# Spectral layers 2 and 3: wider matmuls for two tiles, a turned x transform, 1 MB transfers on two queues, another hand-written order

## The chip, the cores and the metric

The kernel runs on one core of a Trainium2 chip. The metric is the device time of one launch in microseconds, lower is better. All arithmetic is fp32. Engines are named as in the profile: PE is TensorE's matmul stream (PEld its weight loads), DVE is VectorE, ACT is ScalarE, POOL is GpSimd and SP is SyncE. DMA transfers are issued by SP, POOL or ACT and carried by the core's 16 DMA engines.

## The reference

64 images of 256x256 pass a Fourier neural operator of four layers with 32 channels. Its result, 256 tokens of 256 values, gets 77 text tokens appended, and one transformer layer follows (attention, then a feed-forward over about half of the tokens). The change touches only the operator's layers, so the rest is left out:

```python
v = jnp.transpose(h @ p_w + p_b, (0, 3, 1, 2))
for i in range(4):
    W1 = fw1[i, ..., 0] + 1j * fw1[i, ..., 1]
    W2 = fw2[i, ..., 0] + 1j * fw2[i, ..., 1]
    x1 = _fourier_layer(v, W1, W2)       # rfft2, mix 24 x 12 modes over channels, irfft2
    x2 = jnp.einsum('bcxy,cd->bdxy', v, w_w[i]) + w_b[i][None, :, None, None]
    v = x1 + x2
    mean = jnp.mean(v, axis=(0, 2, 3), keepdims=True)
    var = jnp.var(v, axis=(0, 2, 3), keepdims=True)
    v = (v - mean) * jax.lax.rsqrt(var + BN_EPS) * bn_g[i] + bn_b[i]
    if i < 3:
        v = jax.nn.relu(v)
out = jnp.einsum('bcxy,cu->bxyu', v, q_w) + q_b
```

The mean and variance run over all 64 images, so a layer can't be normalised before its whole batch is known.

## The kernel before

The feature map v of an image is 8 MB and goes through HBM between layers. A layer is split in two. `mix` multiplies the few kept Fourier modes by the layer's weights, finds mean and variance from them and from sums of squares, and writes the mixed modes to HBM (`mix_d`). Then `layer(i, ...)` is a pass over the 64 images: it builds the layer's output, applies the normalisation and ReLU, and in the same sweep takes the forward transform of the result and the sums of squares of the next layer. There are three such passes (i = 0, 1, 2; "pass 1, 2, 3" below). Pass 1 needs no feature map as input (it is linear in x); passes 2 and 3 load it. After them the transformer stage loads the map once more.

An image is eight tiles t = 0..7 of 128 partitions (four groups of 32 channels) by 8 rows by 256 columns, 1 MB each. In a pass these steps run, each a small function of `layer`:

- `ld` loads a tile into one of four `vin` buffers: two DMAs on SP, 512 KB each (L661). `am` loads an image's mixed modes into `ams` (two DMAs on SP, L626) and scales them with two POOL instructions (L634).
- `sp` (two halves of an image) turns the modes into rows by a matmul (L667); `spT` transposes them on DVE (L675).
- `pre` makes a tile: eight matmuls of 24 rows from the modes (L687) and sixteen 32x32 ones from `vin` (L698) into four PSUM banks. `evA` and `evB` each evict two of the banks with ReLU into one of four `vo` buffers, on ACT (suffix `.a`, L710) or on DVE (`.d`, L712).
- `st` stores the tile from `vo` to HBM: two DMAs on SP, 512 KB each (L719). `turn` transposes it on DVE into `t32` (L724).
- `prod` multiplies the tile by the next layer's channel weights: sixteen 32x32 matmuls, row group n into bank n (L735). `sqA`, `sqB` square and sum the result on ACT (L746).
- `y0`..`y7`, after all eight tiles of an image, transform along y (L757); `half` (ACT, L767), `zt0` and `zt1` (DVE, L775) carry the result out. `x` transforms along x in twelve matmuls (L791), `xo` copies on ACT (L802), `xs` stores the modes on SP (L808).

PSUM is four pairs of banks, `ring0` to `ring3`. `take` gives the pairs that were closed earliest in program order, `close` marks the step that frees one. `pre`, `prod` and `y` take two pairs, `sp` and `x` one; `y` holds its two from `y0` until `half` and `zt0`.

What sets the order is a string written out by hand, `ORDER[0]` for pass 1 and `ORDER[1]` for passes 2 and 3: a loop over images b emits the steps word by word, `@k` shifts a word to image b + k. No scheduler moves them (`manual_schedule`), so each engine and each queue executes its steps in the order of the string, and waits where its inputs or buffers are not ready. A buffer of `vo` is free again when its tile's store, `turn` and `prod` are done, one of `vin` when its `pre` is done. DMAs of one issuing engine share eight completion semaphores in turn, so a DMA also waits for the one issued eight before it.

Of the kernel before, what the change touches and what calls it, by code (L numbers as in the profile page):

```python
# [9 lines left out]
F32 = mybir.dt.float32  # L10
# [7 lines left out]
C = 32  # L18
M = 12
KX = 2 * M  # L20
# [14 lines left out]
def _tables():  # L35
# [92 lines left out]
ORDER = [(  # L128
# [7 lines left out]
), (  # L136
# [7 lines left out]
)]  # L144

_TABLES, _GRIDS = _tables()
# [7 lines left out]
def tile_fno_fusion_transformer(ctx: ExitStack, tc: tile.TileContext, a, cst_d, grid_d, out):  # L154
    nc = tc.nc
    x = a["x"].rearrange("b x y o -> b x (y o)")
# [3 lines left out]
    const = ctx.enter_context(tc.tile_pool(name="const", bufs=1))  # L160
# [15 lines left out]
    T4, ID, ONES, CHAN = tab("t4"), tab("ident"), tab("ones"), tab("chan")  # L176

    CROW = tab("crow").rearrange("p (n k) -> p n k", n=4)

    epsc = const.tile([128, 1], F32, name="epsc")  # L180
    nc.vector.memset(epsc, EPS)

# [29 lines left out]
    w4 = [w4all[:, i, :] for i in range(L)]  # L212
# [336 lines left out]
    def layer(i, st, src, dst, acc):  # L549
# [3 lines left out]
        EX, FX = EXL[lay], FXL[lay]  # L553
# [3 lines left out]
        with ExitStack() as cx:  # L557
            def pool(name, bufs, **kw):
# [3 lines left out]
            op, yp, cp, xp, zp, tp = (  # L562
                pool(n, k, reuse_waits="tile")
                for n, k in (("lo", 4), ("ly", 1), ("lc", 1), ("lx", 2), ("lz", 1), ("lt", 6))
            )
# [20 lines left out]
            for n in range(nr):  # L586
# [4 lines left out]
                if n:  # L591
                    nc.vector.tensor_add(a0, a0, a1)
            nc.vector.tensor_copy(ams[1], ams[0])
            ws = cp.tile([128, C], F32, name="ws")
            if i:
                nc.vector.tensor_mul(ws, w4[i], s_)
            if i == 0:
                mv = [ip.tile([128, 4, 4 * S + 8], F32, name="mv") for n in range(2)]
                mv = [t[:, :, 0:4 * S].rearrange("p q (s y) -> p q s y", s=4) for t in mv]
                for t in mv:  # L600
                    nc.sync.dma_start(t, grid_d.rearrange("p (q s y) -> p q s y", q=4, s=4))

            ring, free, clock = {}, [0] * 4, [0]

            def take(key, n):

                clock[0] += 1
                mine = sorted((k for k in range(4) if free[k] >= 0), key=lambda k: free[k])[:n]
                for k in mine:
                    free[k] = -1  # L610
                ring[key] = [(k, pp.tile([128, 2, 512], F32, name=f"ring{k}")) for k in mine]
                return [t for _, t in ring[key]]

            def banks(key):
                return [t[:, n] for _, t in ring[key] for n in range(2)]
# [6 lines left out]
            y_, t32, vin, vo, half_, zts = {}, {}, {}, {}, {}, {}  # L622

            def load_am(b):
                for n in range(2):
                    nc.sync.dma_start(  # L626
                        ams[b % 2][64 * n:64 * n + 2 * KX],
                        mix_d[i][:, :, :, b].rearrange("p m k c -> (p m k) c")[:, 512 * n:512 * n + 512],
                    )

            def scale_am(b):
                for _, p0, cs in halves:
                    v = ams[b % 2][p0:p0 + 2 * KX].rearrange("p (c k) -> p c k", k=32)
                    nc.gpsimd.tensor_tensor(  # L634
                        v, v,
                        s_[p0:p0 + 2 * KX, cs].rearrange("p (c o) -> p c o", o=1)
                        .to_broadcast([2 * KX, 16, 32]), ALU.mult,
                    )
# [7 lines left out]
            def am(b, n, e):  # L646
                if b > 1:
                    load_am(b)
                    scale_am(b)

            def lx(b, n, e):
# [3 lines left out]
            def ld(b, t, e):  # L655
                if (b, t) in vin:
                    return
                vin[b, t] = ip.tile([128, 8, S], F32, name="vin")
                for n in range(2):
                    rows = slice(4 * n, 4 * n + 4)  # L660
                    nc.sync.dma_start(vin[b, t][:, rows], src[b][:, t, rows])  # L661

            def sp(b, h, e):
                ps = take(("sp", b, h), 1)[0]
# [49 lines left out]
                return run  # L714

            def st_(b, t, e):
                for n in range(2):
                    rows = slice(4 * n, 4 * n + 4)
                    nc.sync.dma_start(dst[b][:, t, rows], vo[b, t][:, rows])  # L719
# [9 lines left out]
            def prod(b, t, e):  # L729
                take(("prod", b, t), 2)  # L730
                ps = banks(("prod", b, t))
                for k in range(4):
                    for n in range(4):
                        j = (n + k) % 4
                        nc.tensor.matmul(  # L735
                            ps[n][32 * j:32 * j + 32], lhsT=w4[i + 1][32 * n:32 * n + 32],
                            rhs=vo[b, t][32 * n:32 * n + 32, 2 * j:2 * j + 2, :], start=True, stop=True,
                            skip_group_check=True, tile_position=(32 * n, 32 * j),
                        )

            def sq(n):
                def run(b, t, e):
                    key = "prod", b, t
                    at = 2 * (8 * b + t) + n
                    ps = ring[key][n][1]
                    nc.scalar.activation(ps, ps, AF.Square, accum_out=acc[:, at:at + 1])  # L746
                    close(key, n)
                return run
# [21 lines left out]
            def zt(h):  # L770
                def run(b, n, e):
                    if b not in zts:
                        zts[b] = zp.tile([128, 2, 32, C], F32, name="zt")
                    whole = h == 0 or b not in half_
                    nc.vector.transpose(  # L775
                        zts[b][:, h].rearrange("p k c -> p c k"),
                        (ring["y", b][h][1] if whole else half_[b]).rearrange("p n (s c) -> p c (n s)", c=C),
                    )
                    if whole:
                        close(("y", b), h)  # L780
                return run

            def x_(b, n, e):
                zt_ = zts.pop(b)
                ps = take(("x", b), 1)[0]
                for g in range(3):
                    n = 0
                    for h in range(2):
                        for r in range(2):
                            k0 = M * r + 4 * g  # L790
                            nc.tensor.matmul(  # L791
                                ps[:, 0, 96 * g:96 * g + 96],
                                lhsT=zt_[:, h, k0:k0 + 4, :].rearrange("p k c -> p (k c)"),
                                rhs=FX[:, h, 48 * r:48 * r + 96], start=n == 0, stop=n == 3,
                            )
                            n += 1

            xos = {}

            def xo(b, n, e):  # L800
                xos[b] = xp.tile([128, 3, 2 * KX], F32, name="xo")
                nc.scalar.copy(  # L802
                    xos[b], ring["x", b][0][1][:, 0, 0:288].rearrange("p (g k) -> p g k", g=3)[:, :, 0:2 * KX]
                )
                close(("x", b), 0)

            def xs(b, n, e):
# [1 line left out]

            run = dict(  # L810
                am=am, lx=lx, ld=ld, sp=sp, spT=spT, pre=pre, evA=ev(0), evB=ev(1), st=st_, turn=turn,
                prod=prod, sqA=sq(0), sqB=sq(1), y=y, half=half, zt0=zt(0), zt1=zt(1), x=x_, xo=xo, xs=xs,
            )
            steps = []
            for word in ORDER[min(i, 1)].split():
                word, _, late = word.partition("@")
                word, _, e = word.partition(".")
                name = word if word in run else word.rstrip("0123456789")
# [53 lines left out]
    src = vd[L % 2]  # L872
# [50 lines left out]
    with tc.tile_pool(name="tw", bufs=1) as tp, tc.tile_pool(name="tq", bufs=2, space=PSUM) as tq:  # L923
# [5 lines left out]
        for dh in range(2):  # L929
            ps = tq.tile([128, D], F32, name="wtp")  # L930
# [5 lines left out]
        for l, r, d_ in ((wn["q"], wn["k"], wqk), (wn["v"], woT, wvE[:, :, 0:D])):  # L936
            for dh in range(2):
                ps = tq.tile([128, D], F32, name="wtp")
# [21 lines left out]
    rows = [128, 128, TXT]  # L960
# [283 lines left out]
```

## Time and profile before

| what | us |
|---|---|
| median of three runs | 11274.06 (11268.07 to 11280.38) |
| the profiled execution | 11266.44, its span 11264.7 |
| PE busy in the span | 10600.1 (94%) |
| DVE busy | 8446.4 (75%) |
| ACT busy | 6475.0 (57%) |
| POOL busy | 1448.0 (13%) |

The stages follow one another: the first transform and the first `mix` up to about 180 us, pass 1 to about 2550, a `mix`, pass 2 from about 2620 to 5550, a `mix`, pass 3 from about 5630 to 8550, a last `mix`, and the transformer stage to the end. Shares over the whole span mix these stages, so they say little about one of them; a window of one pass is read instead. PE's busy time counts a matmul until its end, so waits between overlapping matmuls hide in it.

The costliest transfers, from the page's list (size, then median time from issue to landing):

```profile
v<-vo SPq DMA_DIRECT2D x3072, 512.0 KB, 7.9
vin<-v SPq DMA_DIRECT2D x2048, 512.0 KB, 9.0
ch<-v SPq DMA_DIRECT2D x512, 1024.0 KB, 13.9
```

### The profile page before, as it was taken

How to read it: one execution, taken by the hardware profiler on the slowest of the kernel's cores; microseconds unless marked ns; L12 is line 12 of the kernel's file. 1: busy time of each engine (PE TensorE's matmuls, PEld its weight loads, DVE VectorE, ACT ScalarE, POOL GpSimd, SP SyncE). 2: the span in 40 equal slices, each digit the busy share in tenths (PEclk: the TensorE clock that was granted, in tenths of full speed). 3: DMA queues.
4: the chain of work that ended last, by engine and by line, in shares of the span. 5: the costliest groups of instructions: out<-in, count | busy, mean ns of one | idle time of the engine just before them, and what ended most of it. 6: DMA issues, size and time to landing. Idle time of an engine off the chain costs nothing.

```text
span 11264.7 us, 409247 instructions
## 1 busy us (share of the span) xinstructions
PE 10600.1 (94%) x182550; PEld 5728.7 (51%) x182550; DVE 8446.4 (75%) x10381; ACT 6475.0 (57%) x10673; POOL 1448.0 (13%) x2179
## 2 busy tenths in 40 slices
PE   6999999998999999999799999999996999999999
PEld 3555555554444444444444444444443666666666
DVE  6888888887777777777677777777776666666665
ACT  5777777775656555566556566556664333333333
POOL 1111111110000000000000000000000333333333
PEclk8999999998999999999999999999998999999999
DMA  6776676678999999999899999999998555555553
GB/s 214 248 248 246 246 249 246 246 252 322 381 383 384 378 379 375 376 379 379 316 366 386 379 376 381 382 380 378 375 379 301 224 228 228 225 226 227 225 227 137
DMA packets 971776, 3457.30 MB, mean 307 GB/s; under 512 B 149016, under 2 KB 198552, under 8 KB 903064
## 3 DMA queue, kind: packets, MB, share of 16 engines
q1 hardware_dynamic: 904576, 3366.80, 77.7%
q0 software_dynamic: 58288, 60.60, 2.3%
q8 instruction: 1429, 23.41, 0.8%
q10 hardware_dynamic: 7144, 3.72, 0.1%
q14 instruction: 339, 2.78, 0.1%
HBM read 1733.60 MB, written 1696.92 MB: 305 GB/s over the span
## 4 chain that ended last, share of the span: by engine, by line
PE 61%; DMA 21%; DVE 9%; ACT 4%; issue 3%; SPq 2%; POOL 0%; ACTq 0%; DVEq 0%; POOLq 0%
PE ring L757 15%; DMA v<-vo 11%; PE ring L687 9%; PE ring L735 8%; DMA vin<-v 6%; PE ring L698 5%; PE hp L992 4%; PE ring L667 3%; PE pp L1155 3%; PE pp L1166 3%; PE ring L791 2%; PE pp L1120 2%; DVE vo L712 2%; PE pp L1185 2%; DMA xh<-xo 2%
## 5 line engine op out<-in xcount | busy, mean ns | idle before, releaser
L746 ACT ACTIVATE ring<-ring 128x1024 f32<-128x1024 f32 x3072 | 3115.9, 1014 | 1176.6 <-PE ring L735 1114.9
L724 DVE STREAM_TRANSPOSE t<-vo 128x2048 f32<-128x2048 f32 x1536 | 3465.4, 2286 | 21.1 <-DVE vo L712 0.9
L735 PE MATMUL ring<-vo,w 32*32 32x512 f32 x49152 | 2401.5, 599 | 80.3 <-ACT vo L710 64.2
L712 DVE TENSOR_SCALAR vo<-ring 128x1024 f32<-128x1024 f32 x1280 | 1543.8, 1221 | 1191.4 <-PE ring L698 805.3
L710 ACT ACTIVATE vo<-ring 128x1024 f32<-128x1024 f32 x1792 | 1792.2, 1023 | 1039.9 <-PE ring L698 498.1
L757 PE MATMUL ring<-t,cst 32*32 32x512 f32 x49152 | 2063.5, 599 | 46.4 <-issue 40.2
L757 PEld LDWEIGHTS ring<-t,cst 32*32 32x32 f32 x49152 | 909.6, 103 | 917.1 <-issue 615.9
L735 PEld LDWEIGHTS ring<-vo,w 32*32 32x32 f32 x49152 | 801.3, 103 | 1064.7 <-issue 397.6
L687 PE MATMUL ring<-cst,y 24*128 24x256 f32 x16384 | 1232.6, 403 | 76.8 <-DVE vo L712 59.5
L634 POOL TENSOR_TENSOR ams<-ams,bns 48x512 f32<-48x512 f32 x384 | 401.1, 1045 | 6964.8 <-DMA ams<-mix 6692.2
L698 PE MATMUL ring<-vin,ws 32*32 32x512 f32 x32768 | 1278.0, 603 | 17.9 <-issue 14.0
L687 PEld LDWEIGHTS ring<-cst,y 24*128 24x128 f32 x16384 | 789.8, 185 | 992.8 <-DVE vo L712 389.1
L675 DVE STREAM_TRANSPOSE y<-ring 128x1024 f32<-128x1024 f32 x384 | 762.7, 1986 | 320.0 <-PE ring L667 319.0
L687 PE MATMUL ring<-mv,y 29*128 29x256 f32 x8192 | 705.1, 403 | 36.6 <-ACT ring L746 20.2
L687 PEld LDWEIGHTS ring<-mv,y 29*128 29x128 f32 x8192 | 455.9, 185 | 370.2 <-ACT ring L746 209.8
L791 PEld LDWEIGHTS ring<-cst,zt 128*128 128x128 f32 x4608 | 533.6, 193 | 176.7 <-ACT vo L710 113.8
L767 ACT COPY half<-ring 128x1024 f32<-128x1024 f32 x192 | 194.5, 1013 | 723.9 <-PE ring L757 723.9
L1193 POOL DMA_DIRECT2D out_dram<-o x1024 | 511.2, 508 | 664.8 <-DVE o L1188 622.9
L746 ACT ACTIVATION_READ_ACCUMULATOR ring<-ring 128x1 f32 x3072 | 585.4, 191 | 0.0
L791 PE MATMUL ring<-cst,zt 128*128 128x96 f32 x4608 | 565.6, 280 | 6.2 <-DVE zt L775 6.0
L775 DVE STREAM_TRANSPOSE zt<-ring 128x1024 f32<-128x1024 f32 x192 | 377.4, 1965 | 242.8 <-PE ring L757 242.8
L667 PE MATMUL ring<-ams,cst 49*128 49x512 f32 (+1 forms) x1536 | 450.4, 641 | 108.7 <-POOL ams L634 40.1
(374 smaller groups left out, 9759.8 us busy)
## 6 DMA issues: line engine op xcount, KB each, us to landing
v<-vo SPq DMA_DIRECT2D x3072, 512.0 KB, 7.9
vin<-v SPq DMA_DIRECT2D x2048, 512.0 KB, 9.0
ch<-v SPq DMA_DIRECT2D x512, 1024.0 KB, 13.9
mix<-ob SPq DMA_DIRECT2D x48, 1024.0 KB, 5.3
ams<-mix SPq DMA_DIRECT2D x384, 96.0 KB, 8.0
xin<-in_x_dram SPq DMA_DIRECT2D x16, 1024.0 KB, 8.2
mv<-in_x_dram POOLq DMA_DIRECT2D x256, 64.0 KB, 7.2
out_dram<-o POOLq DMA_DIRECT2D x1024, 16.0 KB, 3.1
```

The source lines that it names most:

```text
L667: nc.tensor.matmul(ps[:, n, :], lhsT=EX[hv, 128 * h:128 * h + 128], rhs=ams[b % 2][hv], start=True, stop=True, skip_group_check=True,)
L675: nc.vector.transpose(y_[b, h].rearrange("p q c -> p c q"), ring[key][0][1].rearrange("p n (c k) -> p (n c) k", k=32),)
L687: nc.tensor.matmul(ps[n][:, 256 * r:256 * r + 256], lhsT=y_[b, t // 4][32 * n:32 * n + K, q:q + 4, :].rearrange("p q c -> p (q c)"), rhs=m ...
L698: nc.tensor.matmul(ps[n][32 * j:32 * j + 32], lhsT=ws[32 * n:32 * n + 32], rhs=v[32 * n:32 * n + 32, 2 * j:2 * j + 2, :], start=False, sto ...
L710: nc.scalar.activation(to, ring[key][h][1], AF.Relu)
L712: nc.vector.tensor_scalar(to, ring[key][h][1], 0.0, None, ALU.max)
L724: nc.vector.transpose(t32[b, t // 2][:, :, 8 * (t % 2):8 * (t % 2) + 8, :].rearrange("p y s c -> p s y c"), vo[b, t].rearrange("p s (y l) ...
L735: nc.tensor.matmul(ps[n][32 * j:32 * j + 32], lhsT=w4[i + 1][32 * n:32 * n + 32], rhs=vo[b, t][32 * n:32 * n + 32, 2 * j:2 * j + 2, :], st ...
L746: nc.scalar.activation(ps, ps, AF.Square, accum_out=acc[:, at:at + 1])
L757: nc.tensor.matmul(ps[n][32 * j:32 * j + 32], lhsT=FYT[32 * n:32 * n + 32, k, :], rhs=t32[b, j][32 * n:32 * n + 32, k].rearrange("p s c -> ...
L791: nc.tensor.matmul(ps[:, 0, 96 * g:96 * g + 96], lhsT=zt_[:, h, k0:k0 + 4, :].rearrange("p k c -> p (k c)"), rhs=FX[:, h, 48 * r:48 * r + ...
L1193: nc.gpsimd.dma_start(out[b, 64 * n + 16 * g:64 * n + 16 * g + 16].rearrange("(p t) d -> p t d", t=2), o[32 * g + 8 * n:32 * g + 8 * n + 8 ...
```

## The change

Everything is in `layer`, and passes 2 and 3 alone use it; pass 1 keeps its order and its forms.

- A tile is loaded by one 1 MB DMA on SP and stored by one 1 MB DMA on GpSimd's queue.
- The scaling of the modes is a step of its own, `asc`, with its own place in the order; `am` only loads.
- `prod` has a second form, `.w`, used for tiles 6 and 7: eight matmuls of 64x64 with a block-diagonal weight tile `w64`. Each 64-row half n writes a 64-partition half m of bank j.
- `x` has the transform matrix as the stationary operand and the modes as the moving one: four matmuls of 384 columns, whose two halves of y go to separate 64-partition halves of a bank. `xe` copies the result to SBUF on ACT, and `xt` turns and adds the halves with three matmuls against `ID2`, two stacked identities.
- The order is another one: the words are shifted (an image now starts at @0 with its loads and ends at @-2), evictions are divided otherwise between ACT (ten) and DVE (six; before nine and seven), and the steps stand elsewhere.

```diff
 ), (
-    "pre5 sqB7@-1 zt1@-1 sqA7@-1 pre6 evA5.a ld2@1 st4 evB5.d st5 turn4 evA6.a prod5 x@-1 "
-    "evB6.a sqB5 prod6 sqA5 xo@-1 turn5 pre2@1 sqA6 turn6 sqB6 prod4 evA2.a@1 evB2.d@1 "
-    "sqB4 ld0@1 ld7 sqA4 pre0@1 evB0.d@1 ld3@1 prod2@1 st6 evA0.a@1 turn2@1 sqB2@1 sqA2@1 "
-    "pre3@1 ld1@1 evA3.a@1 st2@1 evB3.d@1 pre7 evB7.d prod3@1 ld5@1 evA7.a sqA3@1 turn7 "
-    "pre1@1 st0@1 am@2 sqB3@1 prod0@1 evA1.a@1 evB1.d@1 sqA0@1 st7 sp1@1 st1@1 ld4@1 y0 "
-    "spT1@1 y1 ld6@1 turn0@1 turn3@1 xs@-2 y2 sqB0@1 prod1@1 y3 sqB1@1 sp0@2 y4 sqA1@1 "
-    "spT0@2 y5 y6 st3@1 turn1@1 y7 half.a pre4@1 zt0 prod7 evB4.d@1 evA4.a@1 "
+    "prod3@-1 st7@-2 y3@-2 am@1 sqA3@-1 turn0@-1 turn3@-1 sp0 spT0 sqB3@-1 y4@-2 y5@-2 "
+    "pre6@-1 turn1@-1 evB6.a@-1 st3@-1 evA6.d@-1 y6@-2 ld2 y7@-2 st1@-1 prod6.w@-1 zt0@-2 "
+    "half.a@-2 pre5@-1 zt1@-2 sqA6@-1 sqB6@-1 pre2 ld4@-1 evB5.d@-1 evA5.a@-1 ld7@-1 "
+    "prod1@-1 asc@1 evA2.a evB2.d st6@-1 sqA1@-1 turn6@-1 sqB1@-1 ld3 pre4@-1 ld0 "
+    "evA4.a@-1 evB4.d@-1 pre7@-1 prod4@-1 evB7.a@-1 evA7.d@-1 turn7@-1 x@-2 st2 sqB4@-1 "
+    "turn4@-1 sqA4@-1 turn5@-1 st5@-1 prod5@-1 turn2 xe.a@-2 sqA5@-1 sqB5@-1 xt@-2 prod2 "
+    "xo@-2 st4@-1 sqA2 ld1 pre0 sqB2 evB0.a evA0.a pre3 sp1 evA3.a evB3.a spT1 prod0 sqA0 "
+    "sqB0 pre1 ld6 xs@-2 evA1.a y0@-1 ld5 evB1.d st0 prod7.w@-1 sqB7@-1 y1@-1 sqA7@-1 "
+    "y2@-1 "
 )]
...
+    ID2 = const.tile([128, 2 * KX], F32, name="id2")
+    nc.vector.tensor_add(ID2, ID[:, 0:2 * KX], ID[:, 64:64 + 2 * KX])
...
+            w64 = cp.tile([128, 2, C], F32, name="w64")
+            nc.vector.memset(w64, 0.0)
+            for n in range(4):
+                nc.vector.tensor_copy(w64[32 * n:32 * n + 32, n % 2, :], w4[i + 1][32 * n:32 * n + 32])
...
+            def asc(b, n, e):
+                if b > 1:
                     scale_am(b)
...
-                for n in range(2):
-                    rows = slice(4 * n, 4 * n + 4)
-                    nc.sync.dma_start(vin[b, t][:, rows], src[b][:, t, rows])
+                nc.sync.dma_start(vin[b, t], src[b][:, t])
...
             def st_(b, t, e):
+                if i:
+                    nc.gpsimd.dma_start(dst[b][:, t], vo[b, t])
+                    return
...
+                if e == "w":
+                    for j in range(4):
+                        for n in range(2):
+                            m = (n + j) % 2
+                            nc.tensor.matmul(
+                                ps[j][64 * m:64 * m + 64], lhsT=w64[64 * n:64 * n + 64],
+                                rhs=vo[b, t][64 * n:64 * n + 64, 2 * j:2 * j + 2, :], start=True, stop=True,
+                                skip_group_check=True,
+                            )
+                    return
...
+                if turned:
+                    for r in range(2):
+                        for h in range(2):
+                            nc.tensor.matmul(
+                                ps[64 * h:64 * h + 64, 0, 0:384], lhsT=FX[:, h, 48 * r:48 * r + 64],
+                                rhs=zt_[:, h, M * r:M * r + M, :].rearrange("p k c -> p (k c)"),
+                                start=r == 0, stop=r == 1, skip_group_check=True,
+                            )
+                    return
...
+            def xt(b, n, e):
+                xe_ = xes.pop(b)
+                for g in range(3):
+                    nc.tensor.matmul(
+                        ring["x", b][0][1][:, 1, 96 * g:96 * g + 2 * KX],
+                        lhsT=xe_[:, 128 * g:128 * g + 128], rhs=ID2, start=True, stop=True,
+                    )
```

More of the change, by code (lines that the diff above doesn't have):

```diff
@@ L593, in layer @@
             nc.vector.tensor_copy(ams[1], ams[0])
+            w64 = cp.tile([128, 2, C], F32, name="w64")
+            nc.vector.memset(w64, 0.0)
+            for n in range(4):
+                nc.vector.tensor_copy(w64[32 * n:32 * n + 32, n % 2, :], w4[i + 1][32 * n:32 * n + 32])
+            w64 = w64.rearrange("p n o -> p (n o)")
             ws = cp.tile([128, C], F32, name="ws")
@@ L601, in layer @@
                     nc.sync.dma_start(t, grid_d.rearrange("p (q s y) -> p q s y", q=4, s=4))
+            turned = "xt" in ORDER[min(i, 1)]
             ring, free, clock = {}, [0] * 4, [0]
@@ L648, in am @@
                     load_am(b)
+                    if i == 0:
+                        scale_am(b)
+            def asc(b, n, e):
+                if b > 1:
                     scale_am(b)
@@ L796, in x_, with xe @@
                             n += 1
-            xos = {}
+            xos, xes = {}, {}
+            def xe(b, n, e):
+                xes[b] = xp.tile([128, 384], F32, name="xe")
+                if e == "a":
+                    nc.scalar.copy(xes[b], ring["x", b][0][1][:, 0, 0:384])
+                else:
+                    nc.vector.tensor_copy(xes[b], ring["x", b][0][1][:, 0, 0:384])
+            def xt(b, n, e):
[5 more added lines that the diff above has]
+                    )
             def xo(b, n, e):
@@ L802, in xo @@
                 nc.scalar.copy(
-                    xos[b], ring["x", b][0][1][:, 0, 0:288].rearrange("p (g k) -> p g k", g=3)[:, :, 0:2 * KX]
+                    xos[b], ring["x", b][0][1][:, int(turned), 0:288].rearrange("p (g k) -> p g k", g=3)[:, :, 0:2 * KX]
                 )
@@ L811, in layer @@
                 am=am, lx=lx, ld=ld, sp=sp, spT=spT, pre=pre, evA=ev(0), evB=ev(1), st=st_, turn=turn,
-                prod=prod, sqA=sq(0), sqB=sq(1), y=y, half=half, zt0=zt(0), zt1=zt(1), x=x_, xo=xo, xs=xs,
+                prod=prod, sqA=sq(0), sqB=sq(1), y=y, half=half, zt0=zt(0), zt1=zt(1), x=x_, xe=xe,
+                xt=xt, xo=xo, xs=xs, asc=asc,
             )
```

## Prediction

> **What bounds the kernel now.** I first asked where the time goes, stage by stage, then what each stage waits for. The start of each image's `half` copy (L767) in the timeline gives the rhythm of the three passes over the feature map. Pass 1 runs from 251 to 2536 us, 36.3 us an image. Pass 2 runs from 2695 to 5543 us at 45.19, and pass 3 from 5707 to 8543 us at 45.01. Only passes 2 and 3 ("later passes", 128 images, 45.10 us on average) are changed; they hold about half of the span. The page's slices of those passes show an engine-like row at its ceiling, the DMA one:
>
> ```profile
> PE   6999999998999999999799999999996999999999
> ...
> DMA  6776676678999999999899999999998555555553
> GB/s 214 248 248 246 246 249 246 246 252 322 381 383 384 378 379 375 376 379 379 316 366 386 379 376 381 382 380 378 375 379 301 224 228 228 225 226 227 225 227 137
> ```
>
> The DMA row says 9 (90% or more) in passes 2 and 3 and 5 to 7 elsewhere. PE also says 9, but everywhere. The window 3000 to 5500 us asked alone (pass 2), and then the last stage, give the queue's share:
>
> ```profile
> q1 hardware_dynamic: 268993, 940.09, 97.2%
> q8 instruction: 400, 6.55, 1.0%
> ...
> q1 hardware_dynamic: 65107, 432.80, 53.6%
> ```
>
> Columns: packets, MB, share of 16 engines. Lines 1 and 2 are pass 2: the 16 DMA engines are occupied 98.2% of the time. Line 3 is 9000 to 11000 us, where the kernel only reads, in 1 MB loads. The waits of pass 2 agree:
>
> ```profile
> SPq L719 <- ACT vo L710: 448.9, 115, 7.7
> SPq L719 <- DMA v<-vo: 295.6, 328, 2.4
> SPq L719 <- DMA vin<-v: 223.7, 257, 2.4
> SPq L661 <- DMA vin<-v: 198.7, 188, 2.7
> SPq L661 <- DMA v<-vo: 150.1, 167, 2.2
> ...
> ACT vo L710 <- DMA v<-vo: 122.9, 86, 3.3
> DVE vo L712 <- DMA v<-vo: 116.9, 86, 3.3
> ```
>
> (us in all, times, longest.) SP, which issues every load and store, stands 868 us of 2500 behind earlier transfers (lines 2 to 5): eight are allowed in flight. Evictions then wait for a `vo` buffer whose store has not landed, 1.6 times an image. The chain of waits holds it too:
>
> ```profile
> PE ring L757 15%; DMA v<-vo 11%; PE ring L687 9%; PE ring L735 8%; DMA vin<-v 6%; PE ring L698 5%; PE hp L992 4%; PE ring L667 3%; PE pp L1155 3%; PE pp L1166 3%; PE ring L791 2%; PE pp L1120 2%; DVE vo L712 2%; PE pp L1185 2%; DMA xh<-xo 2%
> ```
>
> (this line of the page stands behind the shares by engine). How much does PE itself need? From start to next start where nothing waits: a `pre` tile 1.08+1.08 us, a `prod` 1.07 (3.45 for `pre` and `prod` in a row), a `y` step 1.10, `sp` 1.06, `x` 2.85. Eight `pre`, eight `prod`, eight `y`, two `sp`, one `x` in the old order make 41.0 us. So now **DMA is the bound** (44.3 of 45.1 us) and PE has 4 us of slack.
>
> **The change, part by part** (per image of passes 2 and 3).
>
> *Loads and stores of 1 MB.* 16+16 half-megabyte DMAs become 8+8. A partition's run becomes 8 KB instead of 4. Engine time per MB: pass 2, 0.972 x 16 x 2500 / 940.09 = 41.4 us; the last stage, 0.536 x 16 x 2000 / 432.80 = 39.6 us, 4.2% less. Single packet records say the same: 4096 B take 159 ns (mean 168), 8192 B 311 (mean 320). DMA time an image: 256 packets per engine x 0.168 + 1.4 (small transfers, instruction fetch, semaphores) = 44.4 now; 128 x 0.320 + 1.3 = **42.3** after. That is the gain's upper end (-2.1). The lower end takes the slow-packet excess as growing with size (0.329): 43.4 (-1.0). The 1 MB row lies nearest but is reads alone; I take 42.8.
>
> *Stores from GpSimd.* Eight issues an image; the `xh` load, 128 runs per issue like these, took POOL 0.55 us, so 4.4 us on an engine that is busy 2.2 of 45. In its queue the scaling (two 1.05 us instructions, waiting for the `ams` landing) stands after tile 1's store and before tile 6's; the `ams` load is issued a whole image earlier, so it delays nothing. Tile 6's store is then due 12 us later. SP keeps 11 transfers an image (35 now), so its limit of eight in flight no longer binds. Here the Trainium skill ("DMA: Bandwidth & Descriptors", section "Issuing engines are not separate DMA queues") speaks against a gain: whatever engine issues, the same 16 engines serve, and only issue time is saved. By the rule the split is worth 0; by the waits of SP up to 0.8 us, the part of 45.1 in which DMA engines now idle. I take 0 here. Were a GpSimd packet slower (nothing large of this kind stores in this trace; the `xh` load's 4 MB landed in 12.5 us, which is full rate), the gain would vanish.
>
> *`prod6.w`, `prod7.w`.* 16 matmuls of 32x32 become 8 of 64x64. Fewer instructions, but a 512-column fp32 matmul is two records that follow each other by 0.43 us on one tile of the array, whatever its size (the `sp` rows, 49x128, and the 32x32 rows alike). 16 tiles side by side need 2 x 0.43 + 0.2 = 1.07; four tiles with two matmuls each need 4 x 0.43 + 0.2 = **1.92**. So +0.85 each. `prod6.w` hides: the following `pre5` must wait 2.06 us for `zt0` to free its PSUM pair. `prod7.w` doesn't: +0.85 on the path. Here a rule speaks louder: "TensorEngine Tiling (Array Packing)", Gotcha 1, says that different row tiles cannot use one PSUM bank at the same time. In the old form row group n writes bank n alone; in the new one both row halves write bank j, in different partitions. No row here shows that. By the rule each pair serialises, 5 rounds of 0.86 + 0.2 = 4.5 us each; by the rows 1.92. I take 1.92 (the outputs lie in separate partitions) and keep 4.5.
>
> *`x` turned.* 12 matmuls of 0.237 (2.85) become four of 384 columns (two pairs: 4 x 0.32 + 0.2 = 1.5) and three turns (6 records x 0.11 + 0.2 = 0.9): -0.45 on PE, and +0.48 on ACT for the `xe` copy (by the `half` and `xo` copies: 0.16 us + 0.83 ns a column). PE waits for that copy.
>
> *The new order.* PE's own need becomes 41.3 us. But PE shares four PSUM pairs with ACT and DVE, so I walked each engine's queue by hand with the durations above (eviction 1.0 on ACT, 1.22 on DVE, starting 2.4 after its `pre`; squares 1.01 apart, pair free 1.1 after the start; turns 2.28; `zt`, `spT` 2.0), landings left out. From `prod6.w` at 0: `pre5` 2.1, `pre2` 4.3, `prod1` 6.3, `pre4` 8.0, `pre7` 10.2, `prod4` 12.1, `x` 13.6, `prod5` 15.1, `xt` 16.5 (ACT's copy), `prod2` 17.6, `pre0` 18.8, `pre3` 21.0, `sp1` 23.2, `prod0` 24.4 and `pre1` 26.4 (ACT evicts both halves of tiles 0 and 3), `y0` 28.6, `prod7.w` 30.1, `prod3` 34.4, `sp0` 36.8, `pre6` 40.1, next `prod6.w` at **44.5**. The same walk gives 41.8 for the old order, and the trace follows it within 0.7 us up to the first wait for a landing; for pass 1's order it gives 37.1 where 36.3 was measured. So the new chain is 43.7 to 44.5. Landings fit: the tightest store (tile 5, issued at 8.6, buffer wanted at 21.2) has 12.6 us, against 9.0 from issue to landing now; the tightest load (tile 0, issued at 6.4, wanted at 19.9) 13.5.
>
> *Rest.* ID2 and `w64` are a handful of small DVE instructions once per pass, under 3 us in all. The pipeline is half an image deeper, under 5 us at each pass's end. I count +5 together.
>
> **The sum.** The bound moves from DMA (44.4 of 45.1) to the engines' chain (about 44.1, middle of 43.7 and 44.5) with DMA close below at 42.8. Bound and result differ by 0.7 us now; with two near bounds I add 0.3: 44.4. (44.4 - 45.1) x 128 = -90, + 5 = -85 us on the profiled execution (11266.4, span 11264.7): 11182. The median of three (11274.06) lies 8 us above that execution, within their spread; I forecast **11185 us**.
>
> **Rivals.** What cannot be told from no change is 0.2%, about 22 us, or 0.18 us an image.
>
> 1. *Forecast* (44.2 to 44.9 an image: 11160 to 11245). Chance 0.42.
> 2. *More*: the two queues keep DMA engines fed and the walk is as pessimistic as for pass 1: 43.3 to 44.2, so 11040 to 11155. For it, SP's 868 us behind earlier transfers; against it, those engines are 98% busy already. 0.12.
> 3. *Nothing*: DMA relief is real but the chain is 45: within 22 us of now. 0.13.
> 4. *Slower, the PSUM bank*: both `prod.w` serialise at 4.5 us: `prod6.w` then delays `pre5` by 2.4, `prod7.w` its followers by 2.6, so 49.4 an image, near 11,810. It decides from 2.5 us a `prod.w` on. 0.13.
> 5. *Slower, two bounds at once*: stores from GpSimd move no faster than now (44.4 of DMA time) and wait in a second queue, while the chain at 44.5 has lost the 3 us of slack which covers late landings today. About 46.0: 11,380. It decides once a store takes over 12.6 us to land. 0.20.
>
> So faster 0.53, same 0.14, slower 0.33. The range 11,060 to 11,400 leaves out rival 4 and a little at the low end.
>
> **What would show it.** Right: DMA share of passes 2 and 3 falls to about 95 to 97%, the waits `vo <- v<-vo` fall well below 240 us in 2500, the idle before `pre` and `prod` names ACT and DVE, `prod.w` takes 1.9 us. Wrong: evictions still wait for stores; a GpSimd store lands later than 12 us; `prod.w` over 2.5 us; images at 45.1 or more although no landing is late.

## The result, and the profile after

| | before | after |
|---|---|---|
| median us | 11273.67 (4 runs, 11268.07 to 11280.38) | 12015.14 (4 runs, 12009.03 to 12018.35) |
| image in pass 2 / pass 3, us | 45.19 / 45.01 | 50.91 / 50.91 |
| image in pass 1, us | 36.26 | 36.27 |

The ratio is 1.0656, 95% interval 1.064 to 1.0672: the change makes the kernel 741 us slower, where 11185 was forecast. Passes 2 and 3 account for it: 128 images by 5.80 us are 743 us. (Image times are from the starts of consecutive `half` copies, here and below.)

First the slices of the page of after, the rows that were shown of before:

```profile
PE   6999999979989999999789999999999799999999
...
DMA  6666766678888888888788888888888655555553
GB/s 218 245 248 247 249 246 246 246 270 338 337 332 338 334 336 334 334 337 330 288 336 334 337 336 335 341 332 335 334 330 316 261 223 229 223 229 220 232 219 149
```

In passes 2 and 3 the DMA row has gone from 9 to 8 and the rate from about 380 to 335 GB/s. The DMA engines are less busy, and the images are slower. The queues in the window 3000 to 5500 us (packets, MB, share of 16 engines) give the size of that:

```profile
q1 hardware_dynamic: 69637, 424.04, 44.0%
q0 software_dynamic: 56089, 408.39, 41.5%
q8 instruction: 339, 5.55, 0.8%
```

86.3% in all, 98.2% before. So over a whole image throughput isn't the bound any more. The waits of the same window (total us, times, longest) say what is:

```profile
POOL v L731 <- ACT vo L723: 1530.3, 225, 18.6
...
ACT vo L723 <- DMA v<-vo: 258.5, 49, 8.0
PEld ring L680 <- ACT vo L723: 238.7, 49, 7.7
...
PE ring L680 <- ACT vo L723: 194.2, 49, 6.8
```

The first line costs nothing: GpSimd, which issues the stores, is idle until a tile is there. The window holds 49 images. Exactly once in each, an eviction on ACT waits for a store, 5.28 us on average, and then PE (its `sp` step, L680) waits for ACT. Before, there were 172 such waits of 1.4 us in 55 images, partly beside each other; now there is one, alone on the path. The chain of waits agrees (11% before):

```profile
PE ring L783 16%; DMA v<-vo 15%; PE ring L700 10%; PE ring L761 8%; PE ring L711 6%; PE ring L680 4%; PE hp L1043 3%; DVE zt L801 3%; PE pp L1206 2%; PE pp L1217 2%; PE ring L752 2%; PE pp L1171 2%; DMA xh<-xo 2%; PE pp L1236 2%; PE pp L1133 1%
```

Which store is it? The timeline of one image (start, duration, engine and line, then in brackets the idle time before it and what ended it):

```profile
5070.57 1.06 POOL L731 DMA_DIRECT2D v<-vo  x2 [7.91 <-ACT vo L723]
...
5072.51 2.48 SPq L674 DMA_DIRECT2D vin<-v  x2
...
5074.47 0.53 POOL L731 DMA_DIRECT2D v<-vo  x1 [2.83 <-ACT vo L723]
...
5084.24 1.14 PE L711 MATMUL ring<-vin,ws 32*32 32x512 f32 x32
5089.27 2.85 ACT L723 ACTIVATE vo<-ring 128x1024 f32<-128x1024 f32 x3 [6.15 <-DMA v<-vo]
5090.35 0.50 PEld L680 LDWEIGHTS ring<-ams,cst 49*128 49x128 f32 x4 [5.88 <-ACT vo L723]
5090.35 2.08 PE L680 MATMUL ring<-ams,cst 49*128 49x512 f32 x4 [4.97 <-ACT vo L723]
```

The two stores at 5070.57 are tiles 2 and 5, the one at 5074.47 is tile 4. The eviction at 5089.27 is `evB0`. The prediction said that tile 0 takes tile 5's buffer. The semaphores say otherwise: `evB0` waits for the one that the store of **tile 4** signals. It starts 0.10 us after that store has landed in 47 of the 49 images; tile 5's store has landed 4.2 us before (median). In the image shown ACT was free at 5083.1, 8.7 us after that store was issued. Issue and landing around it (from the events of the semaphores; landed is the last of a transfer's 16 signals):

```
               issued    landed
store tile 2   5070.57   5081.01
store tile 5   5071.10   5085.86
load           5072.51   5082.98
store tile 4   5074.47   5089.17
load           5074.68   5087.65
```

Both loads overtake a store that was issued before them. Tile 4's store needs 14.7 us here, 14.0 in the median of the window. The page hides it in an average:

```profile
v<-vo POOLq DMA_DIRECT2D x1024, 1024.0 KB, 10.2
```

By position in the image the median landing of a store lies between 4.3 us (tile 0's) and 14.0 (tile 4's). The late landings fall in a burst: seven 1 MB transfers are issued between 5066.7 and 5074.7, and one (a load, at 5083.2) from then until 5091.5.

### The profile page after: what moved, and what is told of

It is laid out like the page before. It is cut to its first block, busy times and chain, and to the rows that moved or that the text cites. A ratio compares the mean times of both kernels' runs of the same rounds, so it can differ in the third digit from the quotient of the medians.

```text
span 12016.6 us, 395176 instructions
## 1 busy us (share of the span) xinstructions
PE 11001.2 (92%) x177174; PEld 5507.7 (46%) x177174; DVE 8287.1 (69%) x10269; ACT 6641.7 (55%) x10929; POOL 1999.2 (17%) x3203
## 4 chain that ended last, share of the span: by engine, by line
PE 64%; DMA 18%; DVE 10%; issue 4%; ACT 3%; SPq 0%; ACTq 0%; POOL 0%; DVEq 0%; POOLq 0%
PE ring L783 16%; DMA v<-vo 15%; PE ring L700 10%; PE ring L761 8%; PE ring L711 6%; PE ring L680 4%; PE hp L1043 3%; DVE zt L801 3%; PE pp L1206 2%; PE pp L1217 2%; PE ring L752 2%; PE pp L1171 2%; DMA xh<-xo 2%; PE pp L1236 2%; PE pp L1133 1%
## 5 line engine op out<-in xcount | busy, mean ns | idle before, releaser
L723 ACT ACTIVATE vo<-ring 128x1024 f32<-128x1024 f32 x1920 | 1904.3, 1025 | 2240.6 <-PE ring L711 1342.5
L783 PE MATMUL ring<-t,cst 32*32 32x512 f32 x49152 | 2186.2, 604 | 30.6 <-issue 24.9
L725 DVE TENSOR_SCALAR vo<-ring 128x1024 f32<-128x1024 f32 x1152 | 1397.2, 1222 | 996.4 <-PE ring L711 898.4
L761 PE MATMUL ring<-vo,w 32*32 32x512 f32 x40960 | 2031.3, 644 | 30.1 <-ACT vo L723 19.0
L731 POOL DMA_DIRECT2D v<-vo x1024 | 551.8, 541 | 5670.5 <-ACT vo L723 3944.2
L700 PE MATMUL ring<-cst,y 24*128 24x256 f32 x16384 | 1333.5, 419 | 19.8 <-DVE y L688 4.4
L680 PE MATMUL ring<-ams,cst 49*128 49x512 f32 (+1 forms) x1536 | 554.8, 784 | 568.6 <-ACT vo L723 502.6
L761 PEld LDWEIGHTS ring<-vo,w 32*32 32x32 f32 x40960 | 578.0, 106 | 952.3 <-ACT vo L723 368.4
L680 PEld LDWEIGHTS ring<-ams,cst 49*128 49x128 f32 (+1 forms) x1536 | 150.4, 217 | 909.2 <-ACT vo L723 619.7
L752 PE MATMUL ring<-vo,w 64*64 64x512 f32 x4096 | 504.7, 608 | 12.5 <-DVE vo L725 12.5
## 6 DMA issues: line engine op xcount, KB each, us to landing
v<-vo POOLq DMA_DIRECT2D x1024, 1024.0 KB, 10.2
```

The costliest lines, as they stand in the source:

```text
L680: nc.tensor.matmul(ps[:, n, :], lhsT=EX[hv, 128 * h:128 * h + 128], rhs=ams[b % 2][hv], start=True, stop=True, skip_group_check=True,)
L700: nc.tensor.matmul(ps[n][:, 256 * r:256 * r + 256], lhsT=y_[b, t // 4][32 * n:32 * n + K, q:q + 4, :].rearrange("p q c -> p (q c)"), rhs=m ...
L723: nc.scalar.activation(to, ring[key][h][1], AF.Relu)
L725: nc.vector.tensor_scalar(to, ring[key][h][1], 0.0, None, ALU.max)
L752: nc.tensor.matmul(ps[j][64 * m:64 * m + 64], lhsT=w64[64 * n:64 * n + 64], rhs=vo[b, t][64 * n:64 * n + 64, 2 * j:2 * j + 2, :], start=Tr ...
L761: nc.tensor.matmul(ps[n][32 * j:32 * j + 32], lhsT=w4[i + 1][32 * n:32 * n + 32], rhs=vo[b, t][32 * n:32 * n + 32, 2 * j:2 * j + 2, :], st ...
```

## The experiments

Each was one edit to the changed kernel or the kernel before. Ratios are to the runs of the kernel before beside them.

**1. Tile 5's store first.** At this point tile 5's store was still taken for the late one.

```diff
-... evA5.a@-1 ld7@-1 ... turn5@-1 st5@-1 prod5@-1
+... evA5.a@-1 st5@-1 ld7@-1 ... turn5@-1 prod5@-1
```

> The changed kernel with one word of its order moved: tile 5's store stands behind tile 5's last eviction (evA5), ahead of tile 6's and tile 2's store, instead of behind turn5. Theory A (one late store: tile 5's store is issued behind tile 2's in a burst of 7 MB and lands 15 to 18 us later where 12.6 are there) expects the wait of ACT's eviction for a store to fall from 5.3 us an image to under 1, an image at 44.5 to 45.7 us, a time of 11200 to 11350. Theory B (a second queue makes stores as such slow, wherever they stand) expects another store to be late in its place: over 49 us an image, 11800 or more.

12781.59 us, 1.1337 (1.132 to 1.1354), 57 us an image: far worse. Theory A fails. Theory B's figures are met (11800 or more, another store waited for), but not for its reason: on GpSimd's queue tile 6's store, until then issued as soon as its tile was evicted, now stands behind tile 5's, which waits for a later eviction. It lands 11.7 us after its issue (the other tiles' after 5.2 to 16.0); it is late because it is issued late. By the semaphores tile 4's evictions wait for tile 6's store: `evA4` starts 0.10 us after it lands, in all 44 images of the window. The waits of that window:

```profile
ACT vo L723 <- DMA v<-vo: 480.8, 44, 12.5
DVE vo L725 <- DMA v<-vo: 471.1, 44, 12.3
PEld ring L761 <- ACT vo L723: 458.6, 44, 12.0
```

A miss that pointed to the cause: it matters which tile takes whose buffer.

**2. The same stores from SP.**

```diff
-                    nc.gpsimd.dma_start(dst[b][:, t], vo[b, t])
+                    nc.sync.dma_start(dst[b][:, t], vo[b, t])
```

> The changed kernel with the 1 MB stores issued by SP instead of GpSimd, same place in the order. Theory B (the second queue is what makes stores late) expects stores to land in about 9 us and the time to fall to 11300 or less. Theory A (the place in the order) expects no gain: tile 5's store still follows tile 2's by less than 1 us, and loads now also stand behind stores that wait for evictions: 11950 to 12300.

11326.19 us, 1.0046 (1.0031 to 1.0061). 689 of the 741 us are gone, with the order, tile forms and pairing untouched. Theory A falls; theory B's 11300 is missed by 26 us. Tile 4's store now lands in 10.7 us. `evB0` could start 9.3 us after its issue and still waits in 40 of 55 images, but only 1.4 us each time:

```profile
ACT vo L723 <- DMA v<-vo: 54.8, 40, 2.9
```

**3 and 4. The old order with 1 MB transfers**, both kinds (stores on GpSimd), then loads alone:

```diff
-                for n in range(2): ... nc.sync.dma_start(vin[b, t][:, rows], ...)
+                nc.sync.dma_start(vin[b, t], src[b][:, t])
```

> The kernel before, old order and old forms of prod and x, with only the transfers changed: 1 MB loads on SP and 1 MB stores on GpSimd, each in its old place. Theory A (only the new order's place for tile 5's store is at fault) expects the DMA time of 42.8 us an image to show: 44.0 to 45.2 us an image, 11130 to 11290. Theory B (the second queue, or the 1 MB size, is at fault) expects 11500 or more.

> The kernel before with only its loads made 1 MB, still on SP; stores stay two of 512 KB on SP. Theory A: half of the DMA relief, 44.5 to 45.2 us an image, 11200 to 11290. Theory C (a transfer of 1 MB lands later than the first of two halves, and the steps behind it start later): 11300 or more.

11294.57 us, 1.0017 (1.0011 to 1.0024), and 11276.25, 1.0000 (0.9991 to 1.0009). The first lies just above theory A's range and far below theory B's. In the old order, 1 MB transfers with the stores from GpSimd cost 0.2%: the second queue alone isn't the loss. The second lies in theory A's range, but at the time of the kernel before: 1 MB loads alone bring nothing.

**5 and 6. Buffers in rotation**, with the stores on GpSimd and then on SP:

```diff
-            vo[b, t] = op.tile([128, 8, S], F32, name="vo")
+            vo[b, t] = op.tile([128, 8, S], F32, name=f"vo{next(turns) % 4}")
```

> The changed kernel with the four vo buffers handed out in strict rotation (four named buffers in the order of pre) instead of by the pool; nothing else. The trace shows that the pool gave tile 0 the buffer of tile 4, whose store is issued 9.1 us before tile 0's eviction is due and lands after 14.0. In rotation tile 0 takes tile 5's buffer (12.6 us, landing 13.2). Theory D (that pairing is the loss): 44.5 to 45.7 us an image, 11190 to 11340. Theory E (the engines' chain of the new order is itself longer than the walk, the stores only show it): 48 us or more, above 11650.

> As the run before, with the stores issued by SP. One queue serves transfers in their order, two share the engines, so that a store also waits for loads issued after it. Theory D: the store of tile 4 is no longer waited for, 44.3 to 45.3 us an image, 11170 to 11300. Theory F (DMA throughput, 45 us an image, bounds every version): 11260 to 11340 whatever the pairing.

11426.06 us, 1.0133 (1.0118 to 1.0148), and 11257.9, 0.9983 (0.9976 to 0.999). The first lies between its two expectations; the second is in theory D's range, and 2 us off theory F's. This is the pairing that the prediction had assumed, and the first run is what its rival 5 (46.0 us an image, 11,380) would have been: 46.35 and 46.10 us an image, tile 5's store landing in 13.3 and its buffer taken 0.10 us later. From SP hardly any eviction waits for a store. The wait of the first and of the second:

```profile
ACT vo L723 <- DMA v<-vo: 74.3, 48, 4.6
```

```profile
ACT vo L723 <- DMA v<-vo: 1.2, 4, 0.5
```

Run 6 has what the prediction assumed, and stores are hardly waited for. Still it takes 45.07 us an image, as much as before the change (45.10) and 0.6 more than the engines' chain in run 9 below. One wait that is left is that of `sp` for the modes, which POOL scales when they have landed; it comes in 28 of 55 images:

```profile
PEld ring L680 <- POOL ams L644: 30.3, 28, 1.1
```

Whether these 0.5 us an image are the rest was not tried.

**7. Half of the stores left out in pass 3**, pairing as it was:

```diff
+                if i == 2:
+                    nc.gpsimd.dma_start(dst[b][:, t, 0:4], vo[b, t][:, 0:4])
+                    return
```

> The changed kernel, but pass 3 stores only the first half of each tile (rows 0 to 3 of 8); pass 2 is as it was. Half of the store traffic of pass 3 is left out. With 12 MB instead of 16 an image, no landing should be late. The walk of the engines (prediction) expects pass 3 at 43.7 to 44.5 us an image beside pass 2 at 51, 11550 to 11620 in all. Theory E (the chain is longer than the walk) expects pass 3 at 46 or more.

11625.77 us, 1.0308 (1.0292 to 1.0323). Pass 3 takes 44.85 us an image, pass 2 beside it 50.82. That is just above the walk's range, and not yet free: tile 4's half store still lands after 10.6 us, and `evB0` still starts 0.10 us later.

**8. The kernel before in rotation** (the diff of 5).

> The kernel before with its vo buffers in strict rotation, nothing else. Its evictions wait 1.6 times an image for a store (about 4.9 us an image in sum on ACT and DVE, partly beside each other). If the pool's pairing costs it time, 11150 to 11250; if DMA throughput bounds it (theory F), 11260 to 11290; if rotation pairs it worse, above 11300.

11256.71 us, 0.9983 (0.9977 to 0.999), between the first two of its expectations. The waits for stores more than halve (57.1 on ACT and 39.8 us on DVE; 122.9 and 116.9 before, which are 4.3 us an image in sum, not 4.9), the time hardly moves. So those waits mostly lay beside other limits.

**9 to 11. The engines without late landings**: rotation and half of the stores of pass 3, for the new order, for the new order with plain `prod` of tiles 6 and 7, and for the old order.

```diff
-prod6.w@-1 ... prod7.w@-1
+prod6@-1 ... prod7@-1
```

> The changed kernel with its vo buffers in rotation (stores on GpSimd), and pass 3 storing only rows 0 to 3 of each tile: half of the store traffic of pass 3 is left out, so that no landing should be late there and pass 3 shows the engines' chain alone. The prediction's walk expects 43.7 to 44.5 us an image in pass 3, beside 46.2 in pass 2. If the chain itself is longer than the walk: 45.0 or more.

> As the run before, with prod6.w and prod7.w as sixteen 32x32 matmuls again. By the prediction prod6.w is hidden behind zt0 and prod7.w costs 0.85 us on the path: pass 3 is 0.8 to 0.9 us an image shorter than in the run before, about 43.5. If the PSUM pairs or ACT set the end there too, less than 0.4.

> The kernel before with its vo buffers in rotation, and pass 3 storing only rows 0 to 3 of each tile, in one 512 KB transfer: half of the store traffic of pass 3 is left out. If the DMA engines bound the kernel before, as the prediction says, pass 3 falls to the walk's 41.8 us an image (41.3 to 42.8). If the engines' chain bounds it, 44.5 or more.

One run each: 11312.03, 11364.02 and 11195.6 us. Pass 3 takes **44.48**, 44.75 and **44.07** us an image: the first in the walk's range, the second not shorter than that, as the prediction's reading had it, but longer, the third between its two expectations and nearer to the one for the chain. In the first two no eviction there waits for a store, in the third one does (2.8 us in 2200). A window of pass 3 of the third run, then one of the first (us, busy time of PE, PEld, DVE, ACT and POOL, granted clock, DMA share, GB/s), show that DMA has room there (0.81 and 0.78) while PE is busy for 97 and 99% of the time:

```profile
6200.00:8400.00 2200.00, 2128.62 (x46167) 1037.74 (x46164) 1697.09 (x944) 1360.35 (x2137) 104.34 (x100) 1.00 0.81 294
```

```profile
6400.00:8400.00 2000.00, 1975.13 (x39706) 827.84 (x39682) 1471.06 (x807) 1285.62 (x2016) 282.77 (x444) 1.00 0.78 290
```

The new order's chain is what the prediction's walk gave (44.5). The old order's isn't: 44.07 against 41.8. And the `.w` form costs nothing there; without it the image is 0.27 us longer (0.4 in pass 2 of the same two runs), not 0.85 shorter.

**12. The old order in rotation with 1 MB loads and stores, all on SP.**

> The kernel before with its vo buffers in rotation and loads and stores of 1 MB, all on SP. If 1 MB transfers relieve the DMA engines (the prediction's 42.8 against 44.4 us of DMA time an image) and the chain is 41.8, it falls to 43.2 to 44.6 us an image, 11040 to 11220. If DMA throughput is the same for both sizes, 45.0 us an image, 11230 to 11290.

11274.1 us, 0.9998 (0.999 to 1.0007), 45.14 us an image. Its queues and stores:

```profile
q1 hardware_dynamic: 142155, 940.85, 94.2%
q8 instruction: 401, 6.57, 1.0%
...
v<-vo SPq DMA_DIRECT2D x440, 1024.0 KB, 12.1
```

The relief is real: 95.2% of 45.14 are 43.0 us of DMA time an image, where the prediction had 42.8. It buys nothing. A 1 MB store lands after 12.1 us; the 9.0 of before is for a half, and the two halves of a tile need 10.2 us from the first issue to the last landing. The store that is waited for, tile 2's, lands no later than in run 8 (12.6 us, 13.0 there), but tile 1's evictions still wait for it, 0.8 us on ACT and 0.4 on DVE. And PE waits more for loads; first run 8, then this run:

```profile
PEld ring L698 <- DMA vin<-v: 9.5, 22, 0.9
```

```profile
PEld ring L696 <- DMA vin<-v: 36.6, 46, 1.5
```

What each of these waits is worth was not separated.

**13 and 14. One queue or two?** The pool's pairing again, with the two queues exchanged, then with everything on GpSimd:

```diff
-                nc.sync.dma_start(vin[b, t], src[b][:, t])
+                (nc.gpsimd if i else nc.sync).dma_start(vin[b, t], src[b][:, t])
```

> The changed kernel, pool's pairing kept, with the two queues exchanged: loads on GpSimd, stores on SP. Theory G (two queues share the DMA engines, so a store also waits for loads issued after it, whoever issues it): tile 4's store still lands 13 us or more after its issue, 50 us an image or more, 11900 to 12100. Theory H (GpSimd's queue serves its transfers more slowly than SP's): the store lands in 9 to 11 us, 45.3 to 46.5 us an image, 11300 to 11450.

> The changed kernel, pool's pairing kept, with loads and stores both on GpSimd, one queue in the order of the string as with both on SP (11326). Theory G (it is one queue against two that counts): tile 4's store lands in about 11 us, 11300 to 11450. Theory H (GpSimd's queue is slow): 11900 or more.

12327.15 us, 1.0938 (1.0918 to 1.0958), and 11390.55, 1.0105 (1.009 to 1.012). Tile 4's store lands in 17.4 us in the first (beyond theory G's range for the time) and in 10.3 in the second. GpSimd's queue is not the slow one: all on it is 1.1% off the kernel before, and SP's stores beside GpSimd's loads are slower than the change itself. Theory H falls. What moves between the issue and the landing of tile 4's store (means over the window 3000 to 5500 us, from the records of the DMA packets) shows how far theory G holds:

| queues | 1 MB transfers issued before it and not landed | MB moved until it lands | GB/s meanwhile |
|---|---|---|---|
| two (after) | 4.0 | 5.5 | 411 |
| two exchanged | 4.0 | 6.7 | 409 |
| one (SP) | 3.2 | 4.2 | 416 |
| one (GpSimd) | 3.1 | 4.1 | 412 |

The DMA engines are no slower; more is moved before the store is done. A part of it is loads that were issued after the store, as theory G says: in after 2.0 loads are under way at its issue and 2.8 MB of loads move, in run 13 2.0 and 3.6. A load issued later lands before 72 of the window's 390 stores in after and 89 of 372 in run 13, and before none of 439 and 433 in runs 2 and 14. Another part stands ahead of it already (4.0 against 3.2 and 3.1); why more is under way with two queues was not separated. Tile 5's store in runs 5 and 6 has as much ahead of it with two queues as with one (3.0 and 3.2), and still 5.1 MB move before it lands, against 4.1. Here too the page's averages over all stores hide the one that counts; of run 13, then of run 14, in the window 3000 to 5500 us:

```profile
v<-vo SPq DMA_DIRECT2D x372, 1024.0 KB, 9.6
```

```profile
v<-vo POOLq DMA_DIRECT2D x434, 1024.0 KB, 10.4
```

The runs with full traffic in one table; "lands" and "taken" are counted from the issue of the store whose buffer `evB0` takes:

| queues, pairing | buffer of tile | lands | taken | us an image (mean of passes 2, 3) | us |
|---|---|---|---|---|---|
| two, pool (after) | 4 | 14.0 | 14.1 | 50.91 | 12015 |
| two exchanged, pool | 4 | 17.4 | 17.5 | 53.33 | 12327 |
| one (SP), pool | 4 | 10.7 | 10.8 | 45.57 | 11326 |
| one (GpSimd), pool | 4 | 10.3 | 10.4 | 45.94 | 11391 |
| two, rotation | 5 | 13.3 | 13.4 | 46.23 | 11426 |
| one (SP), rotation | 5 | 11.4 | no wait | 45.07 | 11258 |

Neither cause alone makes the loss. The pairing costs 68 us with one queue and 589 with two; the second queue costs 168 us in rotation and 689 with the pool's pairing; together they cost 757 (11258 to 12015).

## Why the prediction was wrong, step by step

- **The step that failed is "Landings fit"**: "the tightest store (tile 5, issued at 8.6, buffer wanted at 21.2) has 12.6 us, against 9.0 from issue to landing now". Both terms were wrong. The pool doesn't hand out the four buffers in rotation: tile 0 gets tile 4's, whose store is issued 12.1 us after `prod6.w` starts (in the image shown), so that 9.1 us were there by the walk, 8.7 in that image. And the landing isn't 9.0 but 14.0, that of this very store, in the burst of that order, with two queues. The 9.0 was a median over all stores of before, and over 512 KB halves: in the kernel before, a whole tile already took 10.2 us from its first issue to its last landing in the median, and tile 2's 12.8. 14.0 less 8.7 is 5.3, the wait that the trace has once in each image.
- **"Stores from GpSimd ... I take 0"** failed as well, and feeds the second term. The rule quoted holds in that the same engines serve both queues (409 to 416 GB/s while that store is under way, with one queue or two). That the choice touches issue time only does not hold here: the second queue cost 168 us in rotation and 689 with the pool's pairing. The same page of the Trainium skill ("DMA: Bandwidth & Descriptors", section "Queues, rings and completion order") says that each DMA engine takes turns between the queues that have work. The runs agree: in one queue tile 4's store is never overtaken (10.3 and 10.7 us), in two it also waits for loads issued after it (14.0 and 17.4).
- **Rival 5 had the mechanism, at 0.20.** Its threshold of 12.6 us was that of tile 5's pair; with that pairing (run 5) it comes out at 46.2 us an image against 46.0. What made 11,380 into 12,015 is the pairing, which no rival had.
- **"DMA is the bound" and "PE has 4 us of slack"**: the slack was wrong. With half of the stores of pass 3 gone the old order still takes 44.07 us an image, so relief from DMA was worth 1.0 us at most; DMA time (44.3) and the engines' chain were two near bounds from the start. This is why the forecast gain fails even where landings fit: run 6 takes 11258 us, where 11185 was forecast. The walk's 41.8 for the old order had been compared with the trace only up to the first wait for a landing. What it misses there was not tried.
- **DMA time 42.8** was right for the old order (43.0 in run 12), and no gain came of it beside a chain at 44.1. In the changed kernel it was not: 86.3% of 50.91 are 43.9 us. There an 8 KB packet takes 335 ns on average, 326 in run 12, where 320 were read from the last stage.
- **The chain of 44.5** was met (44.48 in run 9), in part by luck: the same walk is 2.3 us short for the old order, and it counts 0.85 us for `prod7.w` that run 10 does not find on the path. Right, too, were the parts that could be read from rows: a `prod.w` takes 1.95 us from first start to last end (1.92 forecast), `x` 1.51 and `xt` 0.87 us (1.5 and 0.9). The PSUM rival falls (4.5 us by the rule that the prediction quotes, 1.95 measured): two row halves writing one bank in different partitions run at the rate of the rows. The 0.85 us put on the path for `prod7.w` was hidden (run 10); which wait covers it was not separated.

The signs named for "wrong" were the right ones: evictions that still wait for stores, and a GpSimd store that lands later than 12 us.

## What to carry to other kernels

Ask of each buffer which earlier tile it comes from in the order as built, not as a rotation would have it, and set the issue time of that tile's own store against its own landing in its burst; a median over all stores (10.2 us here) doesn't hold for the one on the path (14.0). Two queues are not a faster queue: they let later loads be served beside an urgent store, so split traffic only where the tightest buffer has slack for it. A busy share of 98% is no proof that everything else has slack: take some of the traffic away in one pass and see what the image then takes (45.1 to 44.1 here). And compare landings of the same size: of a whole tile with a whole tile, not with a half. Of the versions that store everything, the fastest (runs 6 and 8) lie 0.17% below the kernel before.

## What the hardware showed that was not expected

The wait costs PE more than its length. Windows of after around the image shown (us, PE busy, granted clock, DMA share, GB/s; a packet counts where it starts, so a share can read 1.01):

```profile
5076.00:5084.00 8.00, 8.00 (x142) 1.00 1.01 412
5084.00:5089.00 5.00, 1.38 (x38) 0.90 0.97 398
5089.00:5093.00 4.00, 2.65 (x20) 0.50 0.20 82
5093.00:5097.00 4.00, 4.00 (x93) 0.77 1.01 387
5097.00:5101.00 4.00, 4.00 (x81) 1.00 1.01 352
```

After 4.97 us without work PE starts again at half of its clock (0.50 up to 5093, 0.77 on average from there to 5097); the `sp` step at 5090.35 takes 2.08 us, where the prediction read 1.06 in the trace of before. Over pass 2 the granted clock is 0.94 in after, and 1.00 in before and in runs 6 and 9. From the start of `sp` to the start of `prod7.w` an image takes 8.15 us in after and 6.76 in run 5 (means of pass 2). These 1.4 us come on top of the wait; the lower clock fits them, and nothing else was tried. The DMA columns of the same rows show the other side: while the eviction waits, all that was issued lands but for one load, and when it is served the DMA engines have run nearly dry (share 0.20 from 5089 to 5093). The late store delays the engines, and the engines then leave DMA idle, which is how a share of 86% and a kernel held up by one store go together.
